# A retention layer with a mixture of experts on one Trainium2 core: the first step reordered over the engines, half-expert weights issued by ScalarE, and the tile numbers of the first groups computed in one part

## The chip, the cores and the metric

The kernel runs on one core of one Trainium2 chip. The metric is device time in microseconds (us); below, it is the median of several executions. A core has TensorE (PE; its weight loads are shown apart as PEld), VectorE (DVE), ScalarE (ACT), GpSimd (POOL) and SyncE (SP). Each engine works through its own list of instructions in order. Transfers are issued by SP, ACT or POOL, each on a queue of its own, and are carried by 16 DMA engines.

## The reference

For `x` of 2 x 2048 tokens and 256 features, in float32:

```python
x = x + attn(layernorm(x))      # gated linear attention, 4 heads of 64, decay per head
x = x + moe(layernorm(x))       # 8 experts, the best 2 of each token, 256 -> 1024 -> 256
```

The attention keeps a state W per head. With y the normalised input, v = y W_write^T, and y shifted by one token as the key, each chunk gives `reads = (y y_shifted^T * M) v + (W y) * g_p`, where M, g_p, g_w and g_C are powers of gamma = sigmoid(decay). The reads are scaled by alpha = exp(log_alpha), multiplied by W_read^T and added to the residual. The second part takes a softmax over 8 gate logits, picks the two best experts, and adds `p * (gelu(x w1 + b1) w2 + b2)` for each.

## The kernel before

**Order.** Everything is scheduled by hand: the order of the program text is the order of each engine's list. `attention(p)` (lines 404 to 510) is a generator for step p of 16; a step handles 128 tokens of both sequences. It yields seven times (k = 0 to 6), and the main loop (lines 920 to 940) puts other work into these places. From step 9 on the expert tiles are woven in; each `piece()` is one eighth of a tile of 128 token slots. After the 16 steps only tiles are left, so most of the kernel's time is the two matmul lines L853 (`ph`, first expert matrix) and L815 (`py`, second).

**One step.** On PE: `pv` (L414, values and gate logits from the transposed input yT), `pS` (L423, scores), `pO` of the step before (L392, the product with W_read), `pt` (L341, transposes for the next step), `pR` (L467 and L475, reads), `pW` (L495, the state's change). On DVE: `A` = pS times the decay mask (L429), the statistics of step p + 2 (L277 to L231), the addition of pO (L395), the new state (L500), `rg` (L354). On ACT: the copies v (L416), yT (L347) and rdT (L480), `wkg` (L365), the sum x (L322) and, for steps 1 to 10, the normalised y (L297). POOL raises the variance to the power -0.5 (L233), makes the masks and writes token rows to their experts' slots in DRAM (L523). SP moves y into the shifted copy wk (L309 to L311) and loads the next xin (L84).

**Start (lines 87 to 149 and 869 to 883).** xin(0), wwT and xin(1) are loaded by SP; decay, log_alpha, gateT, wrT and wr by ACT. The log decay needs an Exp and a Ln on ACT and small operations on DVE (L121 to L137); from it ACT makes the mask dmask (L140, four Exps), g_w, g_c and g_p (L146 to L149), and POOL cuts the mask (L142). `ps` (L872) sums the gate weights, and L876 centres them. Then come the statistics, y and transposes of step 0, the statistics of step 1, the rest of the mask, the sum x of step 0, `setup_rest` (lines 174 to 203, constants on POOL and three transfers on ACT) and the scaling of wrg by alpha (L883). `norm(1)` stands inside step 0, behind A.

**Expert weights.** The second matrices w2 stay in SBUF. SP issues them in 16 halves of 512 KB (L925), up to a count per step, `W2_BY = [2, 5, 8, 11, 14, 16]`. The first matrices w1c, 1 MB a tile, are loaded per tile by `ask_weights` (L753), and the token rows xg by `ask` (L764); both read the tile's numbers (expert and row) from SBUF into a register of SP first.

**Routing.** `route(q)` (L529) is a generator for a group of two steps. It yields 1 inside a woven part, whose next operation may be put anywhere between DVE's other operations by `beside()` (L251), and yields nothing at the end of a part. `advance()` (L886) finishes the woven part and starts the next. `dispatch(q)` (L679) computes the numbers of the tiles that are full after group q: 14 small DVE operations in five parts, one between each pair of slot writes. `EARLY` gives 9 tiles for q = 1, 8 after that. The tiles of a group are known to `ask_weights` when dispatch has ended, and to `ask` when the route has.

**PSUM.** The pool ps_m has three buffers that pv, pW, pK (L613), pg, ph and, from result 7 on, pO take in turn; whoever takes a buffer waits for the reader of the one before.

Of the kernel before, what the change touches and what calls it, by code (L numbers as in the profile page):

```python
# [46 lines left out]
def block_kernel(  # L47
# [68 lines left out]
    left = iota(one([P, 1], F32, "left"), [[0, 1]], P - 1, -1)  # L116

# [10 lines left out]
    nc.vector.tensor_scalar(neg, neg, 0.0, None, ALU.max)  # L128
    nc.vector.tensor_scalar(age, age, 0.0, None, ALU.max)

    def decays():

        nc.vector.tensor_scalar(lg, lg, 1.0, None, ALU.add)
        nc.scalar.activation(lg, lg, AF.Ln)
        yield
        nc.vector.tensor_tensor(lg, lg, neg, ALU.add)
        nc.vector.tensor_scalar(lg, lg, -1.0, None, ALU.mult)  # L137
        nc.vector.tensor_scalar(g_w, lg[:, 0:H], left, None, ALU.mult)
        for h in range(H):
            nc.scalar.activation(dmask[:, h % 2, h // 2, :], age, AF.Exp, scale=lg[:, h : h + 1])  # L140
        dmask4 = dmask.rearrange("p j g c -> p (j g) c")
# [4 lines left out]
        nc.scalar.activation(g_w, g_w, AF.Exp)  # L146
        nc.scalar.activation(g_c, lg[:, 4:6], AF.Exp, scale=float(P))
        for hh in range(2):
            nc.scalar.activation(g_p[:, hh, :], pos, AF.Exp, scale=lg[:, 4 + hh : 5 + hh])  # L149
        yield  # L150
# [23 lines left out]
    def setup_rest():  # L174
# [5 lines left out]
        nc.scalar.dma_start(slots[DUMMY : DUMMY + SB, :], empty)  # L180
        nc.scalar.dma_start(out[N : N + SB, :], empty[:, :D])
# [4 lines left out]
        )  # L186
        iota(ebase, [[RB, E]], 0, 0)
# [15 lines left out]
        nc.scalar.dma_start(b1_sb, b1)  # L203
# [80 lines left out]
    def norm(p):  # L284
# [10 lines left out]
        for b in range(B):  # L295
            if 0 < p < EASY + 2:
# [107 lines left out]
    def attention(p):  # L404
# [29 lines left out]
        if first:  # L434
            norm(1)
# [216 lines left out]
    def whole(n_f, n, name, ef, row, pick):  # L652
# [6 lines left out]
        yield  # L659
# [11 lines left out]
        yield  # L671
# [7 lines left out]
    def dispatch(q):  # L679

        n = EARLY[q]
        if not n:
# [8 lines left out]
        yield  # L691
# [4 lines left out]
        yield from whole(n_f, n, str(q), ef, t_row, hot)  # L696
        nc.vector.tensor_copy(t_e, ef)
        yield
# [311 lines left out]
```

## Time and profile before

| | |
|---|---|
| median of 5 executions | 647.01 us |
| lowest, highest | 644.19, 648.09 us |
| the profiled execution | 644.14 us |
| its span, first to last instruction | 642.4 us |
| time around the span | 1.74 us |
| mean granted TensorE clock | 0.991 of full speed |

The span is divided among the steps like this; the times are the starts of the first pv of each step.

| step | 0 | 1 | 2 | 3 | 4 | 5 | 6 | 7 | 8 | 9 |
|---|---|---|---|---|---|---|---|---|---|---|
| start of pv, us | 8.61 | 19.50 | 27.07 | 34.64 | 42.68 | 51.20 | 60.05 | 68.61 | 77.12 | 85.75 |

In the page, an engine's busy time stands beside its share of the span. A row of the timeline has the start, the duration, the engine, the line and the operation, the tile written and those read, and in brackets how long the engine had been idle and what ended that. A row of the windows has the busy time of each engine in a stretch of the span, the granted clock, the mean busy share of the DMA engines and the rate.

### The profile page before, as it was taken

How to read it: one execution, taken by the hardware profiler on the slowest of the kernel's cores; microseconds unless marked ns; L12 is line 12 of the kernel's file. 1: busy time of each engine (PE TensorE's matmuls, PEld its weight loads, DVE VectorE, ACT ScalarE, POOL GpSimd, SP SyncE). 2: the span in 40 equal slices, each digit the busy share in tenths (PEclk: the TensorE clock that was granted, in tenths of full speed). 3: DMA queues.
4: the chain of work that ended last, by engine and by line, in shares of the span. 5: the costliest groups of instructions: out<-in, count | busy, mean ns of one | idle time of the engine just before them, and what ended most of it. 6: DMA issues, size and time to landing. Idle time of an engine off the chain costs nothing. (4 is left out here: it accounts for less than half of the span.)

```text
span 642.4 us, 14995 instructions
## 1 busy us (share of the span) xinstructions
PE 619.5 (96%) x4706; PEld 561.8 (87%) x4706; DVE 261.4 (41%) x1141; ACT 288.9 (45%) x770; POOL 223.5 (35%) x198
## 2 busy tenths in 40 slices
PE   5999989999999999999999998999999999999995
PEld 3877779998999999999999998999999999999994
DVE  4588986346443464524542552222222222222220
ACT  5787763435334353434434443444444444443441
POOL 4016676416531256213641671211121122111121
PEclk9899989999999999999999999999999999999998
DMA  4789698946876567566766688776777667777741
GB/s 134 261 275 334 167 355 224 281 139 181 243 210 192 146 170 230 156 196 195 181 199 179 194 255 261 223 195 186 194 212 214 196 187 194 216 214 186 191 99 20
DMA packets 58720, 129.77 MB, mean 202 GB/s; under 512 B 7968, under 2 KB 43936, under 8 KB 50064
## 3 DMA queue, kind: packets, MB, share of 16 engines
q1 hardware_dynamic: 44384, 110.46, 56.7%
q0 software_dynamic: 12720, 17.47, 12.8%
q10 hardware_dynamic: 1536, 0.84, 0.4%
q8 instruction: 42, 0.69, 0.4%
q14 instruction: 38, 0.31, 0.2%
HBM read 101.54 MB, written 23.01 MB: 194 GB/s over the span
## 5 line engine op out<-in xcount | busy, mean ns | idle before, releaser
L853 PEld LDWEIGHTS ph<-xT,w1c 128*128 128x128 f32 x2144 | 317.3, 192 | 25.8 <-DVE xT L791 1.2
L853 PE MATMUL ph<-xT,w1c 128*128 128x128 f32 x2144 | 328.7, 276 | 1.0 <-DVE xT L791 1.0
L858 ACT ACTIVATE hT<-ph,b1c 128x128 f32<-128x128 f32 x536 | 196.8, 367 | 295.2 <-PE ph L853 293.1
L815 PE MATMUL py<-w_sb,hT 128*128 x1072 | 319.7, 380 | 0.0
L822 POOL DMA_INDIRECT out<-yo,dest x67 | 105.4, 1573 | 320.8 <-DMA out<-yo,dest 84.9
L815 PEld LDWEIGHTS py<-w_sb,hT 128*128 128x128 f32 x1072 | 163.0, 192 | 0.2
L821 DVE SCALAR_TENSOR_TENSOR yo<-py,wt,b2c 128x256 f32<-128x256 f32 x67 | 32.3, 483 | 240.4 <-PE py L815 238.8
L523 POOL DMA_INDIRECT slots<-pay,slot_i x64 | 63.2, 987 | 43.7 <-ACT wkg L365 15.7
L414 PE MATMUL pv<-wwg,yT 128*128 128x264 f32 x128 | 34.7, 412 | 3.1 <-DVE state L500 2.3
L392 PE MATMUL pO<-wrg,rdT 128*128 128x264 f32 x128 | 33.2, 392 | 0.0
L414 PEld LDWEIGHTS pv<-wwg,yT 128*128 128x128 f32 x128 | 24.4, 199 | 8.8 <-PE pv L414 3.5
L429 DVE TENSOR_TENSOR A<-pS,dmask 128x1024 f32<-128x1024 f32 x16 | 19.6, 1223 | 29.7 <-PE pS L423 29.7
L789 PE MATMUL px<-ident,xg 128*128 128x128 f32 x134 | 25.8, 275 | 3.7 <-DMA xg<-slots 3.0
L791 DVE COPY xT<-px 128x256 f32<-128x256 f32 x67 | 27.8, 415 | 1.8 <-PE px L789 1.7
L789 PEld LDWEIGHTS px<-ident,xg 128*128 128x128 f32 x134 | 18.8, 142 | 10.8 <-issue 2.1
L392 PEld LDWEIGHTS pO<-wrg,rdT 128*128 128x128 f32 x128 | 23.7, 190 | 4.4
L395 DVE TENSOR_TENSOR x<-x,pO 128x264 f32<-128x264 f32 x32 | 13.4, 426 | 31.5 <-PE pO L392 31.5
L803 DVE TENSOR_SCALAR b2c<-b2c,wt 128x256 f32<-128x256 f32 x67 | 24.6, 367 | 2.4
L233 POOL TENSOR_TENSOR rstd_a<-ve_a,expo 128x2 f32<-128x2 f32 x16 | 13.1, 819 | 27.7 <-DVE ve_a L231 16.0
L423 PEld LDWEIGHTS pS<-yT 64*128 64x128 f32 x256 | 15.6, 187 | 5.9 <-issue 3.5
L553 ACT ACTIVATE pay<-x,shift_b,rstd_b 128x256 f32<-128x256 f32 x32 | 19.0, 594 | 2.3 <-DVE shift_b L238 2.1
L500 DVE SCALAR_TENSOR_TENSOR state<-state,g_c,pW 128x128 f32<-128x128 f32 x30 | 9.2, 343 | 23.3 <-PE pW L495 23.0
(163 smaller groups left out, 430.7 us busy)
## 6 DMA issues: line engine op xcount, KB each, us to landing
w1c<-in_w SPq DMA_DIRECT2D x67, 1024.0 KB, 7.1
xg<-slots SPq DMA_DIRECT2D x67, 132.5 KB, 7.0
b2c<-in_b SPq DMA_DIRECT2D x67, 128.0 KB, 4.8
w_sb<-in_w SPq DMA_DIRECT2D x16, 512.0 KB, 5.4
xin<-in_x SPq DMA_DIRECT2D x16, 256.0 KB
out<-x SPq DMA_DIRECT2D x16, 256.0 KB, 2.2
wk<-y SPq DMA_DIRECT2D x16, 224.0 KB, 6.2
out<-yo,dest POOLq DMA_INDIRECT x67, 6.7
```

The source lines that it names most:

```text
L392: nc.tensor.matmul(pO, lhsT=rdTs[p][:, c, b * P : (b + 1) * P], rhs=wrg[:, c, :], start=(c == 0), stop=(c == 1))
L414: nc.tensor.matmul(pv, lhsT=yT[:, b, c, 1:], rhs=wwg[:, c, :], start=(c == 0), stop=(c == 1))
L429: nc.vector.tensor_tensor(A, pS.rearrange("p j (b g) -> p j b g", b=B), dmask.rearrange("p j g c -> p j (g c)").unsqueeze(2).to_broadcast( ...
L523: put = nc.gpsimd.indirect_dma_start(out=next(slot_views), out_offset=IndirectOffsetOnAxis(ap=index, axis=0), in_=rows, in_offset=None,)
L789: nc.tensor.transpose(px[:, c, :], xg[:, c * P : (c + 1) * P], ident)
L791: nc.vector.tensor_copy(xT, px)
L803: nc.vector.tensor_scalar(b2c, b2c, wt, None, ALU.mult)
L815: nc.tensor.matmul(r["py"], lhsT=hT, rhs=w2_sb[:, ds(r["at"], 1), fc * D : (fc + 1) * D].rearrange("p a d -> p (a d)"), start=(fc == 0), s ...
L821: nc.vector.scalar_tensor_tensor(yo, r["py"], r["wt"], r["b2c"], ALU.mult, ALU.add)
L822: add = nc.gpsimd.indirect_dma_start(out=next(out_views), out_offset=IndirectOffsetOnAxis(ap=r["dest"], axis=0), in_=yo, in_offset=None, c ...
L853: nc.tensor.matmul(ph, lhsT=r["w1c"][:, c, fc * P : (fc + 1) * P], rhs=r["xT"][:, c, :], start=(c == 0), stop=(c == 1),)
L858: mark[0] = nc.scalar.activation(hT, ph, AF.Gelu_apprx_tanh, bias=r["b1c"][:, fc : fc + 1]).ins.name
```

## The change

Seven things are changed. (1) The first loads are spread anew: xin(0) goes in two halves, one on SP and one on ACT; gateT stands ahead of decay and log_alpha on ACT; wrT and wr go to SP. (2) The decay's arithmetic moves: |decay| by an Abs on ACT in place of two DVE operations, the "+ 1" as the bias of the Ln, the clamp of `age` on POOL, and two DVE operations of the log become one. The Exps of g_w, g_c and g_p come ahead of POOL's cut of the mask. (3) `norm(1)` comes ahead of step 0, with y(1) on DVE, and the second call of `decays` ahead of the transposes of step 0. (4) `setup_rest` is split, and the sum x of step 0, the second half of the setup, the scaling of wrg and three transfers come inside step 0; the transfers go to SP. (5) 14 matmuls of the identity, whose result is not read, are put on PE: ten ahead of ps and four behind it. (6) The w2 halves are issued by ACT, from k = 4 of step 0 on. (7) The numbers of the tiles of q = 1, 2 and 3 are one woven part.

```diff
-    xins = {0: load_x(0)}
+    xins = {0: chk.tile([P, B, D], F32, tag="xin", name="xin_0", bufs=4)}
+    nc.sync.dma_start(xins[0][:, 0, :], x[0, 0:P, :])
+    nc.scalar.dma_start(xins[0][:, 1, :], x[1, 0:P, :])
+    nc.sync.dma_start(wwg[:, :, :D], wwT.rearrange("(c p) o -> p c o", p=P))
+    nc.scalar.dma_start(wwg[:, :, D:], gateT.rearrange("(c p) e -> p c e", p=P))
     nc.scalar.dma_start(dec, decay)
     nc.scalar.dma_start(lal, log_alpha)
-    nc.sync.dma_start(wwg[:, :, :D], wwT.rearrange("(c p) o -> p c o", p=P))
-    nc.scalar.dma_start(wwg[:, :, D:], gateT.rearrange("(c p) e -> p c e", p=P))
     xins[1] = load_x(1)
-    nc.scalar.dma_start(wrg[:, :, :D], wrT.rearrange("(c p) o -> p c o", p=P))
-    nc.scalar.dma_start(wr_sb, wr.rearrange("(c p) o -> p c o", p=P))
+    nc.sync.dma_start(wrg[:, :, :D], wrT.rearrange("(c p) o -> p c o", p=P))
+    nc.sync.dma_start(wr_sb, wr.rearrange("(c p) o -> p c o", p=P))
...
+    nc.gpsimd.tensor_scalar(age, age, 0.0, None, ALU.max)
...
-    nc.vector.tensor_scalar(neg, dec, -1.0, None, ALU.mult)
-    nc.vector.tensor_tensor(mag, dec, neg, ALU.max)
+    nc.scalar.activation(mag, dec, AF.Abs)
     nc.scalar.activation(lg, mag, AF.Exp, scale=-1.0)
     nc.scalar.activation(alpha, lal, AF.Exp)
-    nc.vector.tensor_scalar(neg, neg, 0.0, None, ALU.max)
-    nc.vector.tensor_scalar(age, age, 0.0, None, ALU.max)
+    nc.scalar.activation(lg, lg, AF.Ln, bias=1.0)
 
     def decays():
-        nc.vector.tensor_scalar(lg, lg, 1.0, None, ALU.add)
-        nc.scalar.activation(lg, lg, AF.Ln)
-        yield
-        nc.vector.tensor_tensor(lg, lg, neg, ALU.add)
-        nc.vector.tensor_scalar(lg, lg, -1.0, None, ALU.mult)
+        nc.vector.tensor_scalar(neg, dec, -1.0, 0.0, ALU.mult, ALU.max)
+        yield
+        nc.vector.scalar_tensor_tensor(lg, lg, -1.0, neg, ALU.mult, ALU.subtract)
         nc.vector.tensor_scalar(g_w, lg[:, 0:H], left, None, ALU.mult)
...
-            if 0 < p < EASY + 2:
+            if 1 < p < EASY + 2:
                 nc.scalar.activation(
...
         beside()
-        if first:
-            norm(1)
         if p + 2 < NC and p < EASY:
             norm_stats(p + 2)
         yield
         scaled_writes(p)
         if first:
+            sums(0)
             gate_products()
...
+        pause = 1 if 2 * (q + 1) < EASY else None
...
-        yield
+        yield pause
...
+    def warm_up(n, name):
+        pm = ps_m.tile([P, P], F32, tag="pm", name=f"warm_{name}")
+        for _ in range(n):
+            nc.tensor.matmul(pm, lhsT=ident, rhs=ident, start=True, stop=True)
+
+    warm_up(10, 0)
     ps = ps_m.tile([P, E], F32, tag="pm", name="ps")
     for c in range(2):
         nc.tensor.matmul(ps, lhsT=ones, rhs=wwg[:, c, D:], start=(c == 0), stop=(c == 1))
+    warm_up(4, 1)
     norm_stats(0)
     next(start)
     norm(0)
+    next(start)
     nc.vector.scalar_tensor_tensor(wwg[:, :, D:], by_e(ps, 2), -1.0 / D, wwg[:, :, D:], ALU.mult, ALU.add)
     transposes(0)
+    setup = setup_rest()
+    next(setup)
+    next(start)
     norm_stats(1)
-    next(start)
-    sums(0)
-    setup_rest()
-    for c in range(2):
-        nc.vector.tensor_scalar(wrg[:, c, :D], wrg[:, c, :D], alpha[:, c : c + 1], None, ALU.mult)
+    norm(1)
+
+    def behind_first():
+        next(setup)
+        for c in range(2):
+            nc.vector.tensor_scalar(wrg[:, c, :D], wrg[:, c, :D], alpha[:, c : c + 1], None, ALU.mult)
+        nc.sync.dma_start(slots[DUMMY : DUMMY + SB, :], empty)
+        nc.sync.dma_start(out[N : N + SB, :], empty[:, :D])
+        nc.sync.dma_start(b1_sb, b1)
...
         for k, _ in enumerate(attention(p)):
-            if k in (0, 2, 3, 4) and halves < W2_BY[p]:
+            if p == 0 and k == 0:
+                behind_first()
+            if (p or k > 3) and k in (0, 2, 3, 4, 5) and halves < W2_BY[p]:
                 e, j = divmod(halves, 2)
                 js = slice(j * FC * D // 2, (j + 1) * FC * D // 2)
-                nc.sync.dma_start(w2_sb[:, e, js], w2[e, :, js])
+                nc.scalar.dma_start(w2_sb[:, e, js], w2[e, :, js])
```

The five plain yields between the parts of `dispatch` and `whole` become `yield pause`.

More of the change, by code (lines that the diff above doesn't have):

```diff
@@ L140, in decays @@
             nc.scalar.activation(dmask[:, h % 2, h // 2, :], age, AF.Exp, scale=lg[:, h : h + 1])
+        nc.scalar.activation(g_w, g_w, AF.Exp)
+        nc.scalar.activation(g_c, lg[:, 4:6], AF.Exp, scale=float(P))
+        for hh in range(2):
+            nc.scalar.activation(g_p[:, hh, :], pos, AF.Exp, scale=lg[:, 4 + hh : 5 + hh])
+        yield
         dmask4 = dmask.rearrange("p j g c -> p (j g) c")
@@ L145, in decays @@
         )
[L146 to L149, printed above, removed]
         yield
@@ L179, in setup_rest @@
         nc.gpsimd.tensor_scalar(empty[:, ROW - 1 : ROW], pcol, float(N), None, ALU.add)
-        nc.scalar.dma_start(slots[DUMMY : DUMMY + SB, :], empty)
-        nc.scalar.dma_start(out[N : N + SB, :], empty[:, :D])
         nc.gpsimd.memset(before, 1.0)
@@ L186, in setup_rest @@
         )
+        yield
         iota(ebase, [[RB, E]], 0, 0)
@@ L202, in setup_rest @@
         nc.gpsimd.memset(base_e, 2.718281828459045)
-        nc.scalar.dma_start(b1_sb, b1)
+        yield
     slot_views = iter(dram_disjoint_views(slots, 2 * N // P + E + NTILE))
@@ L650, in block_kernel, with whole @@
     tiles, found, known = [], [], []
-    def whole(n_f, n, name, ef, row, pick):
+    def whole(n_f, n, name, ef, row, pick, pause=None):
         upto = sml.tile([P, E], F32, tag="upto", name=f"upto_{name}")
@@ L670, in whole @@
         nc.vector.tensor_tensor(pick, wide(ef, E), by_e(e_of, n), ALU.is_equal)
-        yield
+        yield pause
         nc.vector.tensor_tensor(tmp, pick, by_e(origin, n), ALU.mult)
@@ L690, in dispatch @@
         nc.vector.tensor_copy(n_f, n_i)
-        yield
+        yield pause
         t_e = one([P, n], I32, f"t_e_{q}")
@@ L695, in dispatch @@
         ef = sml.tile([P, n], F32, tag=f"ef{n}", name=f"ef_{q}", bufs=1)
-        yield from whole(n_f, n, str(q), ef, t_row, hot)
+        yield from whole(n_f, n, str(q), ef, t_row, hot, pause)
         nc.vector.tensor_copy(t_e, ef)
-        yield
+        yield pause
         got = sml.tile([P, E], F32, tag="got", name=f"got_{q}")
```

## The prediction

> **What bounds the kernel now.** I read the engine table first, then the windows, then the timeline of the start and of the step at which the expert tiles begin.
>
> ```profile
> PE 619.5 (96%) x4706; PEld 561.8 (87%) x4706; DVE 261.4 (41%) x1141; ACT 288.9 (45%) x770; POOL 223.5 (35%) x198
> ```
>
> PE is busy for 96% of the span. From the first expert matmuls at 91.50 us it stands idle for 2.5 us (0.7 and 1.8 us before px). So a microsecond saved ahead of 91.5 us comes off the end, as long as the order of PE's list stays; nothing that the change touches makes PE's list after that shorter. The time is to be won in two places. The first is step 0:
>
> ```profile
> 3.96 0.75 DVE L277 BATCH_NORM_STATS2 st<-xin 128x6 f32<-128x256 f32 x2
> 8.61 3.89 PE L414 MATMUL pv<-wwg,yT 128*128 128x264 f32 x8 [0.78 <-DVE yT L344]
> 12.43 1.19 PE L423 MATMUL pS<-yT 64*128 64x128 f32 x16
> 13.73 1.23 DVE L429 TENSOR_TENSOR A<-pS,dmask 128x1024 f32<-128x1024 f32 x1 [3.03 <-PE pS L423]
> 15.71 1.18 PE L341 MATMUL pt<-ident,y 128*128 128x128 f32 x4 [1.11 <-ACT y L297]
> 16.83 1.97 PE L475 MATMUL pR<-A,v 128*64 128x128 f32 x16
> ...
> 19.50 2.05 PE L414 MATMUL pv<-wwg,yT 128*128 128x264 f32 x8
> ```
>
> Step 0 takes 10.89 us from pv to pv (8.61 to 19.50), though step 1 with more work takes 7.57. The reader is to see two things. PE waits for y(1), which is made only behind A; and PE is slow: the eight pv take 3.89 us here and 2.05 at 19.50, pR 1.97 and 1.09 later (33.15). The granted clock of 16 to 19 us is 0.50. It prints as 1.00 before 15 us, yet the durations say half speed there until about 12.4. The second place:
>
> ```profile
> 90.10 0.44 PE L789 MATMUL px<-ident,xg 128*128 128x128 f32 x2 [1.22 <-DMA xg<-slots]
> ...
> 91.50 2.90 PE L853 MATMUL ph<-xT,w1c 128*128 128x128 f32 x12 [0.95 <-DVE xT L791]
> ```
>
> PE waits 1.22 us for the first token rows and 0.95 for xT and its first register load; then the clock of 91 to 95 us is 0.51, 0.50, 0.50, 0.78, which costs 1.7 us (the sum of what is missing).
>
> **The first loads.** The statistics start at 3.96, behind four DVE operations from 3.21 on. Without these they start when xin(0) is there: not before 3.2 (decay, 3 KB, landed 2.4 us after its issue at 0.81), not after 3.96. I take 3.3. From the statistics to the first transpose took 2.75 us (3.96 to 6.71), so pt stands at 6.05 and ends at 7.2.
>
> But decay and log_alpha are now third and fourth on ACT's queue, issued at about 1.70 and 2.15, and alpha's Exp stands ahead of the Ln. From alpha's Exp to the end of Ln took 1.71 us (4.68 to 6.39, a table load of 1.28 in it). Landing 2.4 us after the issue, as decay did, log_alpha is there at 4.55 and Ln is done at 6.3: hidden, because y(0) ends at 6.3. Landing 3.95 us after it, as gateT did (1.74 to 5.69), it is there at 6.1 and Ln is done at 7.8. Then DVE, in order, holds lg, g_w, the centring (0.2 + 0.23 + 0.17) and the copy yT (0.69) behind it, and pv starts at 9.1 where the first case gives 7.95. gateT is the nearest row, a small transfer behind others on this queue, and there are 128 KB more ahead; I weigh it four to one. An Abs was not on ACT before; it costs 0.2 like the Exps beside it, or 1.28 more should it bring a fourth table load. "ScalarE: Activation LUTs" of the Trainium skill (Table sets: the hidden batching unit) has abs in every set, so no load; no run here shows it.
>
> wrT and wr, behind xin(1) on SP, are first used at some 14 us; everything loaded at the start had come by 6.5 us (the DMA share falls to 0.03 in 7 to 8), so they are hidden, as is the clamp of age on POOL (0.29 like L183, done by 2.5, used after 7).
>
> **From pv to the next pv.** If pv starts at 9.1 and the clock is as before: pv until 13.0, pS until 14.1, A from 14.2 to 15.45. Beside A PE now has pg (1.06) and pt(1) (0.6 at full clock), done by 15.8, since y(1) is early: dmask from the second Exp table's end (7.8 + 1.28) to 10.4, POOL's cut 0.64, the power 0.77, shift and y(1) on DVE 1.0, together 13.0. pR at 15.85 and then 1.49 us to pv as in later steps (33.15 to 34.64): pv(1) at 17.35, 2.15 us sooner. ScalarE is no later: v by 13.8, wkg 1.26, x 1.09, then yT(1) by 16.9. With pv at 7.95 the same sum gives pv(1) at 16.15, 3.35 sooner. Weighed, **-2.4 us**. What hides the rest of the setup is PE: POOL's second half (about 2 us) and DVE's wrg are not waited for before pO at 22.
>
> **The identity matmuls.** Four 128-column matmuls take 1.12 us at the slow clock (6.71), so ten last from 1.5 to about 3.7 and four 0.9 more behind ps. They delay nothing, since gateT lands later. Bounds: 0, or pv at 2.05 instead of 3.89, -1.8. I take 0, the row that exists being pv at half speed after transposes without a gap over 0.8 us.
>
> "TensorE: Matmul & The Clock Gate" of the Trainium skill (Part 1) says that full clock comes after a window of some 3.4 us of sustained work, and that PE falls back after an idle one. Both slow stretches here last about 3.4 us, which agrees; but they follow idle times of only 1.1 and 2.2 us, so the trace is stricter. By the rule ten matmuls with a wait behind them fill no window, and this term is 0; were the rule wrong here it would be -1.8.
>
> **w2 on ScalarE.** SP's 16 issues took 0.47 us each (median), up to 1.01. Three a step add 1.4 us to ACT, which is busy 5.1, 5.3, 7.6, 5.3 and 7.7 us of steps 1 to 5 (7.57, 7.57, 8.04, 8.52, 8.85 long). In even steps ACT waits 1.15 us for pt and 1.05 for pR at just these places: hidden. In step 3 two issues stand ahead of yT(4); 0.4 us go into its wait for L573, and the copy ends at 42.7 instead of 42.1, when pv starts at 42.68. The second half of pv waits there for the state until 44.55 anyway. Cost 0; +1 if the cover goes. SP's list gets shorter, but no PE wait of these steps ends on an SP load.
>
> "Trainium Kernel Development and Optimization" of the Trainium skill (Key Constraints) has it that all issuing queues share the same 16 DMA engines, and that a second one only saves issue time. By that rule neither the split xin(0) nor w2 moves any byte sooner. DMA shares of 0.82 to 0.98 in steps 1 to 5 agree.
>
> **One woven part.** In step 6 the numbers of the first tiles are then known at k = 0 instead of k = 4, ahead of wk(8) and xin(10) on SP, so w1c of tiles 0 and 1 (issued 76.45 and 78.14, 7 us to land) leave some 5 us sooner, into a stretch with a DMA share of 0.09 to 0.45 (70 to 74). xg, issued at 81.9 and 8.2 us on its way, has less ahead of it. The price is on DVE: eleven operations of 0.22 us, 2.4 us, now stand in one go ahead of L395. In step 6 nobody waits. In step 8 pv(9) takes the PSUM buffer of pO(7), whose reader moves from 83.79 to about 86.4:
>
> ```profile
> 83.79 0.42 DVE L395 TENSOR_TENSOR x<-x,pO 128x264 f32<-128x264 f32 x1
> ...
> 85.75 2.05 PE L414 MATMUL pv<-wwg,yT 128*128 128x264 f32 x8
> ```
>
> So pv(9) waits until 86.9, 1.1 us: a new wait in place of the 1.22 us for xg. A(9) and xT follow it, and ph starts 0.5 us later than now, but the idle time is in two pieces. I take it that the slow stretch then goes: +0.5 - 1.7 = **-1.2 us**. Bounds: +0.6 (clock as now) and -3.9 (no idle time and full clock). For q = 3, 14 operations (3.1 us) go in one piece at 105.0, ahead of xT (105.47), which ph needs at some 108.2: **+0.3**, from 0 to 0.5.
>
> **Sum.** -2.4 - 1.2 + 0.3 = -3.3: an execution like the profiled one (span 642.4 and 1.74 around it, 644.14) would take 640.8. The median of the runs, 647.01, stands 2.87 above it, and I let that distance be: 643.7. No change is within 0.5% (3.2 us), about what a measurement of this kernel can tell.
>
> **Rivals.** (1) The Ln chain and the new PSUM wait eat it: pv at 9.6, pv(1) -1.6, clock as now +0.6, q = 3 +0.5: -0.5, 646.5. For it: ACT's order, gateT's 3.95 us. Against: y(1) is off PE's path in any case. (2) Everything early: -3.35 at the start, -1.8 for the warm clock but only -1.0 of that since A waits for the mask, -2.6 at the tiles: -7, 640. For it: decay's 2.4 us. (3) ScalarE is held by its w2 issues: they are in order, ahead of yT, rdT and wkg, while the DMA engines are 0.82 to 0.98 busy. ACT has 9.5 us free in steps 1 to 5 and gets 14 issues; at 1.2 us each they take 16.8, 7.3 too much: +4.0 after the gain, 651. It outweighs the gain from 0.91 us an issue. SP's longest speaks for it, the median of 0.47 against.
>
> **Chances.** Forecast 0.52, rival 1 0.24, rival 2 0.13, rival 3 0.11. The range 640.0 to 648.0 takes in the first three and leaves rival 3 and a tail out. The forecast straddles the 0.5% bound: faster by more, 0.35 of its 0.52 and rival 2, 0.48; slower 0.10; within 0.42.
>
> **What would show it.** pv(1) at 17.4 (right) or 19 (wrong); DVE idle ahead of lg for Ln; pv(0) still 3.9 us long; pv(9) waiting for L395; no clock of 0.50 after the first ph; w2 issues of 0.5 us on ACT, yT not behind them. An xg that lands after PE asks for it, or a clock lost elsewhere, would make the sum wrong.

## The result, and the profile after

The changed kernel takes **648.67 us** (median of 28 runs, 646.10 to 652.55); the kernel before takes 645.95 us (54 runs). The ratio is **1.0048, 95% interval 1.0035 to 1.0061**: slower by about 3.1 us, where I had forecast 3.3 us less. The profiled execution has a span of 649.3 us (642.4 before) and so shows a loss of 6.9 us, more than the typical one. Sizes are therefore taken from ratios below, and places from traces. Line numbers are those of the changed kernel, for most lines one less than before (pv L413, pO L391, A L428, the sum with pO L394); pv(p) is the first pv of step p.

The engine table of the page after:

```profile
PE 624.3 (96%) x4734; PEld 565.6 (87%) x4734; DVE 264.1 (41%) x1138; ACT 288.1 (44%) x769; POOL 225.3 (35%) x199
```

PE has 28 records more (the fourteen identity matmuls, two records each) and still 96%. Nothing in shares and sums tells what happened; it takes the timelines. The first is PE's in step 0, after:

```profile
1.45 4.64 PE L875 MATMUL warm<-ident 128*128 128x128 f32 x20 [1.45 <-POOL ident masks.py:199]
...
9.75 2.05 PE L413 MATMUL pv<-wwg,yT 128*128 128x264 f32 x8 [1.43 <-DVE yT L343]
11.73 1.16 PE L422 MATMUL pS<-yT 64*128 64x128 f32 x16
...
15.06 1.09 PE L473 MATMUL pR<-A,v 128*64 128x128 f32 x16 [0.69 <-ACT yT L345]
...
16.54 2.05 PE L413 MATMUL pv<-wwg,yT 128*128 128x264 f32 x8
```

The first step gained: pv(0) starts 1.1 us later than before (decay landed at 6.46, Ln behind it, yT behind Ln), but it takes 2.05 us instead of 3.89, and pv(1) starts at 16.54 instead of 19.50. The second is ACT's, in steps 1 and 2:

```profile
23.04 0.33 ACTq L945 DMA_DIRECT2D w_sb<-in_w  x1
23.42 0.20 ACT L345 COPY yT<-yT 128x4 f32<-128x4 f32 x1 [1.95 <-DMA wk<-y]
...
26.58 0.34 ACTq L945 DMA_DIRECT2D w_sb<-in_w  x1
26.95 0.59 ACT L478 COPY rdT<-pR 128x512 f32<-128x512 f32 x1 [2.85 <-DMA wk<-y]
```

An issue takes 0.33 us, as small as I said. But ACT was idle for 1.95 and 2.85 us ahead of the two copies, the issue included, until a transfer wk<-y landed that neither the copy of yT nor that of rdT reads: the issue ahead of them waits, and they stand behind it. PE then waits 1.39 us for rdT ahead of pS. The third is PE's in steps 7 to 9:

```profile
77.70 0.67 PE L465 MATMUL pR<-rg,state 64*64 64x128 f32 x16 [0.83 <-DVE A L428]
80.81 0.42 PE L612 MATMUL pK<-both,before 128*128 128x40 f32 x2 [0.52 <-DVE both L590]
...
83.47 1.13 PE L413 MATMUL pv<-wwg,yT 128*128 128x264 f32 x4 [1.01 <-DVE state L498]
88.90 2.13 PE L391 MATMUL pO<-wrg,rdT 128*128 128x264 f32 x4 [2.12 <-ACT v L415]
94.09 2.05 PE L413 MATMUL pv<-wwg,yT 128*128 128x264 f32 x8
98.98 1.60 PE L853 MATMUL ph<-xT,w1c 128*128 128x128 f32 x12 [1.39 <-DVE xT L791]
```

The waits for A and for v are nowhere in the trace of before. From pv(7) to pv(9) it was 17.14 us; now it is 22.78. The wait for v leads to ACT's sums, which waited for the buffer x1 of two groups earlier to be written out:

```profile
86.14 1.09 ACT L321 ACTIVATE x<-xin,shift_a,up 128x256 f32<-128x256 f32 x2 [4.92 <-DMA out<-x]
```

### The profile page after: what moved, and what is told of

It reads as the page before. It is cut to its first block, busy times and chain, and to the rows that moved or that the text cites. A ratio compares the mean times of both kernels' runs of the same rounds, so it can differ in the third digit from the quotient of the medians.

```text
span 649.3 us, 15048 instructions
## 1 busy us (share of the span) xinstructions
PE 624.3 (96%) x4734; PEld 565.6 (87%) x4734; DVE 264.1 (41%) x1138; ACT 288.1 (44%) x769; POOL 225.3 (35%) x199
## 5 line engine op out<-in xcount | busy, mean ns | idle before, releaser
L413 PE MATMUL pv<-wwg,yT 128*128 128x264 f32 x128 | 33.8, 404 | 3.9 <-DVE state L498 2.5
L391 PE MATMUL pO<-wrg,rdT 128*128 128x264 f32 x128 | 35.4, 411 | 2.1 <-ACT v L415 2.1
L428 DVE TENSOR_TENSOR A<-pS,dmask 128x1024 f32<-128x1024 f32 x16 | 19.6, 1224 | 32.3 <-PE pS L422 32.3
L413 PEld LDWEIGHTS pv<-wwg,yT 128*128 128x128 f32 x128 | 23.8, 194 | 9.1 <-PE pv L413 3.6
L391 PEld LDWEIGHTS pO<-wrg,rdT 128*128 128x128 f32 x128 | 24.8, 200 | 7.4 <-ACT v L415 2.5
L394 DVE TENSOR_TENSOR x<-x,pO 128x264 f32<-128x264 f32 x32 | 13.3, 427 | 32.2 <-PE pO L391 32.0
L422 PE MATMUL pS<-yT 64*128 64x128 f32 x256 | 19.5, 294 | 1.4 <-ACT rdT L478 1.4
```

What stands on the lines that cost most here:

```text
L391: nc.tensor.matmul(pO, lhsT=rdTs[p][:, c, b * P : (b + 1) * P], rhs=wrg[:, c, :], start=(c == 0), stop=(c == 1))
L413: nc.tensor.matmul(pv, lhsT=yT[:, b, c, 1:], rhs=wwg[:, c, :], start=(c == 0), stop=(c == 1))
L422: nc.tensor.matmul(pS[:, j, (2 * b + hh) * P : (2 * b + hh + 1) * P], lhsT=yT[r, b, hh, 0:P], rhs=yT[r, b, hh, 1:], start=True, stop=True,)
```

## The experiments

This table holds the starts on PE (us, from the timelines) of kernels that ran where the kernel before took 645 to 646 us. e4, e9 and e17 ran there too and follow below; the profile of e4 is of an execution 8 us over its median (651.85 us). Labels e1 to e18 are those of the runs below.

| kernel | pv(1) | pv(4) | pv(7) | pv(9) | 7 to 9 | first ph | ratio to before (95%) |
|---|---|---|---|---|---|---|---|
| before | 19.50 | 42.68 | 68.61 | 85.75 | 17.1 | 91.50 | 1 |
| after | 16.54 | 43.38 | 71.31 | 94.09 | 22.8 | 98.98 | 1.0048 (1.0035 to 1.0061) |
| e1: after, w2 on SP | 15.62 | 39.38 | 65.31 | 86.76 | 21.5 | 91.66 | 1.0019 (0.9998 to 1.0040) |
| e2: after, not woven | 16.03 | 42.25 | 68.19 | 85.31 | 17.1 | 90.47 | 0.9974 (0.9949 to 1.0000) |
| e3: first step alone | 15.74 | 39.34 | 65.27 | 82.40 | 17.1 | 88.06 | 0.9955 (0.9933 to 0.9977) |
| e11: before, w2 on ACT | 19.90 | 43.25 | 69.68 | 86.81 | 17.1 | 91.97 | 0.9969 (0.9946 to 0.9991) |
| e12: e1, three x1 | 15.50 | 39.73 | 67.24 | 88.64 | 21.4 | 93.84 | 1.0000 (0.9976 to 1.0023) |
| e10: e3, decay first | 14.81 | 38.07 | 64.02 | 81.14 | 17.1 | 86.30 | 0.9946 (0.9921 to 0.9972) |
| e18: e10, woven, weights behind | 14.97 | 39.16 | 65.10 | 84.94 | 19.8 | 90.15 | 1.0018 (0.9990 to 1.0046) |

The runs e5 to e8 and e13 to e16 fell where the kernel before took 661 to 663 us: there PE stands idle in many places without a releaser in the trace (up to 5 us at a time), and the intervals are 0.7 to 0.9% wide. What differed isn't known: under chip number 8 the kernel before took 662.74 us beside e5 to e8 and 646.33 us beside e17 and e18. In the expectations a counted pv is meant by the time in brackets beside it.

### The three parts, taken apart

My theory after the traces was that ACT's waits cost 3 to 5 us and SP's new order the rest.

```diff
-                nc.scalar.dma_start(w2_sb[:, e, js], w2[e, :, js])
+                nc.sync.dma_start(w2_sb[:, e, js], w2[e, :, js])
```

> The changed kernel with the 16 halves of w2 issued by SyncE again, at the same places of the program. Theory (ScalarE is held at its w2 issues, each of which waits until an older transfer that shares its completion counter has landed, and that is mostly a SyncE transfer such as wk<-y): the waits of yT, rdT and the row copy for wk<-y on ScalarE go, the fifth pv starts near 50 us (54.8 in the changed kernel, 51.2 in the kernel before), and the time falls by 3 to 5 us against the changed kernel: ratio to the kernel before 0.997 to 1.000. Rival a (the w2 bytes crowd the DMA engines whichever queue issues them, and a later first step only shows it): no change, ratio 1.004 to 1.006. Rival b (the loss is all in steps 6 to 9, behind the woven part; what ScalarE loses is caught up by then): ratio 1.003 to 1.005 and the ninth pv still near 94 us.

Measured: 1.0019; pv(4) at 39.38 instead of 43.38, pv(5) at 47.90 instead of 54.76, and none of ACT's waits behind a w2 issue. Against the changed kernel this is 0.0029 (1.9 us), at the edge of what the two intervals tell apart: less than the theory's 3 to 5, more than rival a. What came early was given away again between pv(7) and pv(9), the place that rival b names; its figures don't fit (pv(9) at 86.76 and not near 94).

```diff
-        pause = 1 if 2 * (q + 1) < EASY else None
+        pause = None
```

> The changed kernel with the numbers of the first tiles spread over the steps again (no pause of 1 for the early parts); w2 stays on ScalarE. Theory (w1c and b2c of tiles 0 and 1 stand ahead of out<-x of step 5 on SyncE, so the buffer x1 comes free late, and ScalarE's sums, v and pO wait behind it): out<-x is issued some 8 us sooner, ScalarE's wait of 4.9 us for it goes, pO no longer waits 2.1 us for v, and the time falls by 1.5 to 4 us: ratio to the kernel before 0.999 to 1.002. Rival (the eleven operations in one go on VectorE are the loss, SyncE's order is none): the same fall, but out<-x is awaited as before. Rival (the woven part gains, as predicted): the time rises by about 1 us, ratio 1.006.

Measured: 0.9974, 0.0074 (4.8 us) less than the changed kernel, more than any theory gave. The woven part costs most; pv(7) to pv(9) is 17.1 us again, and ACT no longer waits for out<-x.

Both edits together:

> Both undone: w2 on SyncE and the numbers spread, so that only the reordered first step is left of the change. Theory: the second pv starts near 16.5 us (19.5 before), nothing later takes it away, and the time is 2 to 3.3 us under that of the kernel before: ratio 0.995 to 0.997. Rival (the steps up to the first expert tiles are bound by DMA, so that an early first step is given back by 60 us): ratio 0.999 to 1.001 with the ninth pv at 85 us as before.

Measured: 0.9955, 643.08 us. pv(1) at 15.74 and the first ph at 88.06, 3.4 us sooner than before: what the first step wins isn't given back. Going back by the rows, of the 0.0048 the first step has -0.0045 (-2.9 us), w2 on ACT +0.0019 (+1.2 us, alone within the intervals) and the woven part +0.0074 (+4.8 us). Going back over e1 instead of e2, they are +0.0029 and +0.0064 (1.9 and 4.1 us).

```diff
-                nc.sync.dma_start(w2_sb[:, e, js], w2[e, :, js])
+                nc.scalar.dma_start(w2_sb[:, e, js], w2[e, :, js])
```

in the kernel before, and nothing else:

> The kernel before with nothing changed but the queue of w2: ScalarE issues its 16 halves at the places where SyncE did. Theory (ScalarE waits at them): slower by 2 to 5 us, ratio 1.003 to 1.008, with waits of yT, rdT or the row copy behind a w2 issue. Rival (it costs only together with the early first step, when ScalarE has no slack): within 1 us, ratio 0.9985 to 1.0015. My prediction's term for it was 0, or +1 us.

Measured: 0.9961 (0.9938 to 0.9985): faster, which nobody had expected. Again, for the trace:

> The kernel before with w2 on ScalarE and nothing else, a second time, for its trace: it measured 0.9961 (0.9938 to 0.9985), where a loss was expected, and the first profile (650.2 us at a clock of 0.982) doesn't show where 2.5 us are won. If the gain is real: 0.994 to 0.998, and the trace shows an earlier first ph than 91.5 us, since SyncE, free of w2, issues wk and out<-x sooner. If it was chance: 0.998 to 1.003 and pv and ph where they stand in the kernel before.

Measured: 0.9969 (0.9946 to 0.9991). The gain is there twice. Where it is won I can't show: in its trace pv(1) to pv(9) and ph are 0.4 to 1.1 us later than in the profile of before, and that profile (644.14 us) is itself a quick one of its kernel. What can be said is that the issues on ACT cost nothing when the first step is long; with the short one they cost 0.0019 to 0.0029, about as much as the intervals are wide.

### What w2 costs on ScalarE: the issue, or the wait ahead of it

The first step alone, with a copy on ACT at each of the 16 places:

```diff
                 nc.sync.dma_start(w2_sb[:, e, js], w2[e, :, js])
+                nc.scalar.copy(spent, ident)
```

> The first step alone with w2 on SyncE, and on ScalarE, at each place where a half of w2 is issued, a copy of 128x128 into a tile that nobody reads (about 0.35 us, as long as an issue). It computes nothing that the output needs. Theory (the price of w2 on ScalarE is the wait ahead of the issue, not the 16 x 0.35 us that they occupy): within 0.0015 of the first step alone, pv of steps 1 to 4 within 0.3 us of 15.7, 23.3, 30.9, 39.3. Rival (rival 3 of the prediction: the issues' own time): as with w2 on ScalarE, fifth pv 2 to 3 us later.

Measured: 0.9958 (0.9915 to 1.0001); pv(1) to pv(4) at 15.77, 23.34, 30.91, 39.75. Time on ACT of nearly an issue's length (a copy took 0.30 us) costs nothing by pv(3) and 0.4 to 0.6 us at pv(4) (30.88 and 39.34 in e3, 31.08 and 39.18 in e14, the same kernel without copies), and from pv(1) to pv(4) two executions of one kernel differ by as much (23.80 us in e5, 24.26 in e13). Beside it, the same kernel with the issues on ACT:

> The first step and w2 on ScalarE, not woven, a second time. Theory (ScalarE stands at its w2 issues until an older transfer has landed, and the short first step leaves no slack for it): 0.001 to 0.004 more than the first step alone on this chip, and the fourth and fifth pv 1 to 3 us later (30.9 and 39.3 with w2 on SyncE). Rival (w2 on ScalarE gains, as it did alone): 0.002 to 0.004 less than the first step alone.

Measured: 0.9986 (0.9948 to 1.0024); pv(2) to pv(4) at 23.76, 32.16, 41.76: 0.4, 1.3 and 2.0 us later than with the copies, ACT again idle for 2.15 and 2.23 us where an issue stands. The medians can't tell the two apart here; by the traces it isn't the issue's length, as rival 3 of the prediction had it, but the wait. What an issue waits for stands in the program's semaphores, which the trace keeps: the transfers of both queues share eight completion counters, and a transfer waits until the one that had its counter before has landed. For the w2 issue of the changed kernel at 26.58 us, in program order:

```
SP    wk(2) <- y(2)     counter 5   (third transfer on it)   after ACT's y(2)
ACT   half 5 of w2      counter 5   waits until counter 5 shows three landed
ACT   rdT(1)            behind it in ACT's list
```

Counter 5 showed three landed at 26.55 us. Of the sixteen w2 issues in this trace eight start 0.02 to 0.03 us after the landing that they wait for, six times that of an SP transfer and twice that of an earlier half of w2. With w2 on SP (e1, e3) no wait of ACT between 18 and 60 us ends on a transfer; on ACT they hold up PE, through yT and rdT.

The base of these two, again:

> The first step alone, a second time, as the base of the three others on this chip: 0.994 to 0.997 as before (0.9955, 0.9933 to 0.9977). A second ratio over 0.998 would mean that the gain of the first step isn't firm.

Measured: 0.9979 (0.9940 to 1.0019), pv(1) at 15.95. The ratio lies just under the limit of 0.998 that I had set, and the interval holds 1: by itself this run doesn't confirm the gain, though it doesn't speak against 0.9955 either.

In the reordered step w2 also starts later (k = 4 instead of 0). With the early start, on ACT, not woven:

```diff
-            if (p or k > 3) and k in (0, 2, 3, 4, 5) and halves < W2_BY[p]:
+            if k in (0, 2, 3, 4, 5) and halves < W2_BY[p]:
```

> First step reordered and w2 on ScalarE, numbers not woven (ratio 0.9974 so far), but the first two halves of w2 are issued at k = 0 and 2 of the first step as in the kernel before, not at k = 4 and 5. Theory (w2 on ScalarE costs where its issues fall behind a transfer of SyncE that is still on its way, and the later start of w2 in the changed kernel crowds steps 1 to 3): pv of step 4 near 39.5 to 40.5 us (42.25 with the later start, 39.34 with w2 on SyncE), ratio 0.993 to 0.996. Rival (ScalarE is held in steps 1 to 3 in any case now that the first step is short): pv of step 4 still near 42, ratio 0.996 to 0.999.

Measured: 1.0012 (0.9970 to 1.0054); pv(1) 17.55, pv(2) and pv(3) 7.57 us apart, undisturbed, then pv(4) at 42.77. The waits have moved (2.23 us ahead of yT(1), 2.42 us ahead of yT(4)) and not gone: pv(4) is where the rival has it, though the ratio decides nothing.

### What the woven part costs: SyncE's order, or the operations on VectorE

My theory was SP's order: w1c of tiles 0 and 1 now ahead of out<-x(5), whose buffer ACT's sums wait for. The weights behind it again, w2 on SP:

```diff
-            ask_weights_on(stream["piece"] // FC + 2)
+            if p != 6 or k >= 4:
+                ask_weights_on(stream["piece"] // FC + 2)
```

> First step and woven part as in the changed kernel, w2 on SyncE, but the weights of tiles 0 and 1 are asked for only from the place k = 4 of step 6 on, behind out<-x(5), wk(8) and xin(10), as in the kernel before. So the eleven VectorE operations still stand in one piece, and SyncE's order is the old one. Theory (SyncE's order is the loss): 2.5 to 4.5 us less than with the weights ahead (646.97 there), ratio to the kernel before 0.994 to 0.998, as with the first step alone (0.9955); no wait of ScalarE for out<-x. Rival (the burst on VectorE ahead of the sums x is the loss): ratio 1.000 to 1.003 as with the weights ahead.

> First step and woven part, w2 on SyncE, the weights of tiles 0 and 1 asked for behind out<-x(5), wk(8) and xin(10): a second time, beside the first step alone. If SyncE's order is the whole loss of the woven part: within 0.0015 of the first step alone (which was 0.9955), and the ninth pv between 82 and 83.5 us. If the burst on VectorE has a part of it: 0.002 to 0.004 more than the first step alone, ninth pv at 84 us or later.

Measured: 0.9961 (0.9926 to 0.9996) and 0.9952 (0.9911 to 0.9994). That seemed to settle it for SP's order. But pv(7) to pv(9) was 21.5 and 19.8 us in these traces, with 0.8 to 1.0 us of PE's waiting for A still there; and it was 22.3 us in e16 on the same chip as e13, which isn't woven. There something else sets these steps. The other side of the theory, three buffers with the weights ahead:

```diff
-            x1s[q] = grp.tile([P, G, D + E], F32, tag="x1", name=f"x1_{q}")
+            x1s[q] = grp.tile([P, G, D + E], F32, tag="x1", name=f"x1_{q}", bufs=3)
```

> The other side of the same: first step and woven part as in the changed kernel, the weights ahead of out<-x(5) on SyncE, w2 on SyncE, but three buffers for x1 where there were two, so that ScalarE's sums need not wait until out<-x(5) has been read out. Theory (the loss passes through the buffer x1): ScalarE's wait of 5.2 us for out<-x and PE's of 2.4 us for v go, ratio 0.994 to 0.998, though out<-x is as late as with the weights ahead. Rival (the weights' 2 MB crowd the transfers of these steps, or SyncE's stand at the register load holds wk(8) and xin(10)): xin(10) and xg still come late, ratio 0.999 to 1.003.

> First step, woven part and w2 on SyncE, three buffers for x1, a second time, since the first interval (0.9940 to 1.0032) held both theories. Theory (the loss of the woven part passes through the buffer x1 that out<-x frees late): 0.994 to 0.998, no wait of ScalarE for out<-x, ninth pv near 82 to 84 us (86.8 with two buffers, 82.4 without the woven part). Rival (SyncE's later order costs through xin and xg as well): 0.999 to 1.002.

Measured: 0.9986 (0.9940 to 1.0032), and then 1.0000 (0.9976 to 1.0023). ACT's wait for out<-x is gone, and the loss stays: pv(9) is at 88.64, of which the profile loses some 1.7 us to the clock (0.50 from 80 to 82 us), and the ratio is far from 0.9955. The theory falls here. The deciding run, on the best first step and where before took 646 us, has the weights behind and the operations in one piece:

> The first step with decay first, w2 on SyncE, the numbers of the first tiles in one woven part, the weights asked for behind out<-x(5), wk(8) and xin(10). If the burst on VectorE costs nothing: 0.993 to 0.9965, as without it (0.9946, 0.9921 to 0.9972), eighth and ninth pv near 72.5 and 81.1 us. If it costs 1 to 2 us of its own (A, the sums x and with them pv of step 8 wait behind it): 0.996 to 0.999 and the ninth pv at 82.3 us or later.

Measured: 1.0018 (0.9990 to 1.0046) against 0.9946 without weaving: +0.0072, 4.7 us, with SP's order as before; against e17, which ran beside it and isn't woven either, +0.0067. In the medians SP's order has no part that shows (e1 against e3: +0.0064); in the traces pv(7) to pv(9) takes 21.5 us in e1 and 19.8 in e18, so a part of 1.6 us isn't excluded. DVE's timeline in step 6 shows the price. First with the operations in one piece (e18), then spread (e10):

```profile
60.72 1.22 DVE L428 TENSOR_TENSOR A<-pS,dmask 128x1024 f32<-128x1024 f32 x1
...
64.41 0.23 DVE L670 TENSOR_TENSOR tmp<-hot,origin 128x72 f32<-128x72 f32 x1
64.68 0.23 DVE L673 TENSOR_REDUCE first<-tmp 128x9 f32<-128x72 f32 x1
64.94 0.17 DVE L675 SCALAR_TENSOR_TENSOR t_row<-jj,first 128x9 int32<-128x9 f32 x1
...
65.50 0.77 DVE L394 TENSOR_TENSOR x<-x,pO 128x264 f32<-128x264 f32 x2
...
67.17 0.17 DVE L230 TENSOR_SCALAR ve_b<-mv 128x4 f32<-128x4 f32 x1
...
69.66 0.19 DVE L546 TENSOR_TENSOR pL<-x,rstd_b 128x32 f32<-128x32 f32 x1 [0.79 <-POOL rstd_b L232]
...
70.22 1.22 DVE L428 TENSOR_TENSOR A<-pS,dmask 128x1024 f32<-128x1024 f32 x1
```

```profile
59.63 1.22 DVE L428 TENSOR_TENSOR A<-pS,dmask 128x1024 f32<-128x1024 f32 x1
...
62.06 0.42 DVE L394 TENSOR_TENSOR x<-x,pO 128x264 f32<-128x264 f32 x1
...
64.41 0.20 DVE L230 TENSOR_SCALAR ve_b<-mv 128x4 f32<-128x4 f32 x1
...
64.75 0.23 DVE L670 TENSOR_TENSOR tmp<-hot,origin 128x72 f32<-128x72 f32 x1
64.90 0.15 DVE L329 TENSOR_TENSOR std<-ve_a,rstd_a 128x2 f32<-128x2 f32 x1
65.01 0.23 DVE L673 TENSOR_REDUCE first<-tmp 128x9 f32<-128x72 f32 x1
65.16 0.16 DVE L331 TENSOR_SCALAR std<-std 128x2 f32<-128x2 f32 x1
65.28 0.17 DVE L675 SCALAR_TENSOR_TENSOR t_row<-jj,first 128x9 int32<-128x9 f32 x1
...
66.96 0.18 DVE L546 TENSOR_TENSOR pL<-x,rstd_b 128x32 f32<-128x32 f32 x1
...
67.51 1.22 DVE L428 TENSOR_TENSOR A<-pS,dmask 128x1024 f32<-128x1024 f32 x1
```

From A(6) to A(7) it is 9.50 us against 7.88, for the same operations. So it is in every trace of this set: 9.50 or 9.51 in the woven kernels (after, e1, e12, e18), 7.87 to 7.89 in those without weaving (before, e2, e3, e9, e10, e11, e17). Two things make it up.

The first is GpSimd's power, which makes rstd_b from ve_b and for which DVE stands 0.79 us in e18. In e10 it begins 0.29 us after ve_b (at 64.70) and takes 1.04 us, and seven operations of the numbers lie over it. In e18 those are done, and it begins 1.03 us after ve_b (at 68.20), behind a slot write that runs from 67.22, and takes 1.43 us. With the numbers in one part, four slot writes stand on GpSimd between A(6) and the power where three stood. At e10's times the power would be over at 68.5, before DVE has got to L546 at 68.9: so it is the place on GpSimd that costs, and not only the operations that are gone from above it. Why it takes 1.43 us isn't shown.

The second, the other 0.83 us, is the piece itself: each of its operations needs the one before, and they start 0.26 us apart (64.41, 64.68, 64.94). In e10 they do so too (64.75, 65.01, 65.28), but L329 and L331, which need nothing of them, start in between.

PE, in e18:

```profile
71.49 0.67 PE L465 MATMUL pR<-rg,state 64*64 64x128 f32 x16 [0.84 <-DVE A L428]
74.59 0.41 PE L612 MATMUL pK<-both,before 128*128 128x40 f32 x2 [0.53 <-DVE both L590]
...
77.26 1.13 PE L413 MATMUL pv<-wwg,yT 128*128 128x264 f32 x4 [1.01 <-DVE state L498]
...
84.94 2.02 PE L413 MATMUL pv<-wwg,yT 128*128 128x264 f32 x8 [0.96 <-DVE x L394]
```

Step 7 takes 10.0 us instead of 8.5 (A, both and the state late), step 8 takes 9.8 instead of 8.6 (pv(9) waits for L394): 2.7 us, and q = 3 adds a wait of 0.8 us for xT that only the woven kernels have. That is 3.5 us; the three pairs of medians say 4.1 to 4.8, and what makes up the rest isn't shown.

### The first step, and whether more is to be had

The first step alone without the fourteen identity matmuls:

```diff
-    warm_up(10, 0)
...
-    warm_up(4, 1)
```

> The first step alone (w2 on SyncE, numbers not woven), without the fourteen identity matmuls ahead of and behind ps. Theory (they hold the clock up: pv of step 0 took 2.05 us instead of 3.89 in the changed kernel): pv of step 0 takes 3.0 to 3.9 us again and the second pv starts 0.5 to 1.8 us later than 15.7; time +0.5 to +1.8 us, ratio 0.9965 to 0.9985. Rival (my prediction's term of 0: they change nothing): ratio as with the first step alone, 0.9945 to 0.9965.

Measured: 0.9979 (0.9938 to 1.0019), which holds both. The trace, though of its slowest execution (666.23 us), decides for the theory in the first step:

```profile
8.86 3.89 PE L413 MATMUL pv<-wwg,yT 128*128 128x264 f32 x8 [1.05 <-DVE yT L343]
12.67 2.08 PE L422 MATMUL pS<-yT 64*128 64x128 f32 x16
...
17.77 1.60 PE L413 MATMUL pv<-wwg,yT 128*128 128x264 f32 x6
```

pv(0) takes 3.89 us and pS 2.08 again (2.05 and 1.16 with them), and pv(1) starts at 17.77 instead of 15.74 (e3) or 15.95 (e14): the fourteen matmuls are worth 1.8 to 2.0 us, about half of the 3.8 us that e3 wins by pv(1).

Decay first on ACT's queue:

```diff
+    nc.scalar.dma_start(dec, decay)
     nc.scalar.dma_start(xins[0][:, 1, :], x[1, 0:P, :])
     nc.scalar.dma_start(wwg[:, :, D:], gateT.rearrange("(c p) e -> p c e", p=P))
-    nc.scalar.dma_start(dec, decay)
...
-    nc.scalar.activation(alpha, lal, AF.Exp)
     nc.scalar.activation(lg, lg, AF.Ln, bias=1.0)
...
+        nc.scalar.activation(alpha, lal, AF.Exp)
         nc.scalar.activation(g_w, g_w, AF.Exp)
```

> The first step alone, with decay as the first load of ScalarE's queue instead of the third, log_alpha last, and alpha's Exp behind those of the decay. Theory (the statistics, lg and the copy yT on VectorE wait for decay, which landed at 6.5 us in the changed kernel): Ln is done by 6 us, the first pv starts at 7.9 to 8.4 us (8.95 now) and the second 0.4 to 1 us sooner than 15.7; time 0.4 to 1 us less, ratio 0.993 to 0.9955. Rival (xin(0), now behind decay on the queue, is as late as decay was): first pv between 8.7 and 9.5, ratio as with the first step alone.

Measured: 642.31 us, **0.9946 (0.9921 to 0.9972), the fastest kernel here by ratio**; Ln is done at 6.00, pv(0) starts at 8.23 and pv(1) at 14.81, 0.9 us sooner than in e3. The same first step has pv(1) at 14.97 in e18 and 15.16 in e17, that of e3 at 15.41 to 16.44 in the other traces that have it with w2 on SP. The traces show the step; the time alone couldn't tell it from 0.9955. It beats the kernel before and, with its interval, the changed one (1.0035 at least).

With w2 on SP from the first step's k = 0 on:

```diff
-            if (p or k > 3) and k in (0, 2, 3, 4, 5) and halves < W2_BY[p]:
+            if k in (0, 2, 3, 4) and halves < W2_BY[p]:
```

> The first step with decay first (0.9946 so far), w2 on SyncE, numbers not woven, but w2 from k = 0 and 2 of the first step on, as in the kernel before, not from k = 4. Theory (the DMA share is 0.36 between 10 and 20 us and about 1 from 30 to 60 us, so earlier halves take load off the steps that are full): pv of steps 4 and 5 0.5 to 1.5 us sooner than 38.07 and 46.58, ratio 0.992 to 0.995. Rival (these steps aren't held by transfers when SyncE issues w2): pv within 0.3 us of that, ratio 0.9935 to 0.9965. Rival (wk(1) and xin(3) come late behind 1 MB): second pv or the third later than 14.8 and 22.4 by over 0.5 us.

Measured: 0.9951 (0.9922 to 0.9981); pv(1) to pv(9) within 0.4 us of the run without it (pv(0) is 0.8 us later), the first rival. When SP issues w2, it makes no difference where it starts.

Identity matmuls also at the first expert tile, on the first step alone:

```diff
+        if stream["piece"] == 0:
+            ph = ps_m.tile([P, SB], F32, tag="pm", name="ph_0_0")
+            for _ in range(3):
+                nc.tensor.matmul(ph, lhsT=ident, rhs=ident, start=True, stop=True)
...
+            for _ in range(5):
+                nc.tensor.matmul(ph, lhsT=ident, rhs=ident, start=True, stop=True)
```

> The first step alone (w2 on SyncE, numbers not woven), with eight identity matmuls more at the first expert tile: three ahead of px, where TensorE waits for xg (0.83 us in the profile of the first step alone), and five between px and the first ph, where it waits for xT (1.26 us). Theory (short idle times of about 1 us are what takes the clock to half for 3.4 us; work in them keeps it): the first twelve ph take 1.60 us instead of 2.70, no clock under 0.9 between 88 and 92 us, time 1.0 to 1.7 us under the first step alone, ratio to the kernel before 0.9925 to 0.9945. Rival (the clock falls anyway, or the eight delay px and ph): the same or up to 1 us more, 0.9950 to 0.9975.

Measured: 0.9965 (0.9947 to 0.9983), no gain over 0.9955. The clock was 1.00 throughout 84 to 94 us, as the theory has it, and PE lost the time again elsewhere:

```profile
86.87 0.44 PE L789 MATMUL px<-ident,xg 128*128 128x128 f32 x2 [1.04 <-DMA xg<-slots]
88.46 1.38 PE L859 MATMUL ph<-ident 128*128 128x128 f32 x10 [1.15 <-issue]
89.67 1.50 PE L861 MATMUL ph<-xT,w1c 128*128 128x128 f32 x12
```

The five matmuls behind px didn't start until 1.15 us after it, beside the time in which xT was made, and then stood 1.2 us ahead of ph. The first ph starts at 89.67 instead of 88.06.

## Why the prediction was wrong, point by point

**What bounds the kernel: right.** The places were the first step and the tiles' beginning, and PE's idle time and clock there came through to the end (e3: 3.4 us at the first ph, 2.9 us in the median).

**The first loads: right in kind.** I weighed the Ln chain behind decay's load as four to one, with pv(0) at 9.1; it came at 9.75 in the profile of after, at 8.95 in e3 and at 8.23 with decay first. In after decay itself landed at 6.46 us, 4.7 us after its issue, where my nearest row had 3.95; in e3 it was there at 4.72, and log_alpha at 6.04. DVE did idle ahead of lg (1.10 us) for Ln. Three table loads stand on ACT (2.78, 7.06, 8.84), as many as before; Abs uses the one that Exp uses and brings no fourth, so the Trainium skill's "ScalarE: Activation LUTs" (Table sets) agrees with the trace.

**From pv to pv, and the identity matmuls: right sign, two sizes off.** I had -2.4 for the first and 0 for the second. pv(1) came 2.96 us sooner (3.8 in e3). The step that failed is "ten last from 1.5 to about 3.7". The sum was off already, since ten at four in 1.12 us last 2.8 us; and they lasted to 6.09, since each of these float32 matmuls is two records in the trace (ten are x20) and a transpose, from which I took the price, is one (four are x4). So PE worked from 1.45 on, for 4.64 us by these ten alone, and pv ran at full speed. "TensorE: Matmul & The Clock Gate" of the Trainium skill (Part 1) wants some 3.4 us of sustained work. Here the matmuls come 0.21 us apart until 6.4 us in e3 and 6.9 in after, and then 0.11: full speed came 4.9 and 5.5 us after the first, and in e8 PE worked from 8.86 to 14.68, 5.8 us, before it came. None of these traces has it after less than 3.4 us, and it was my length that made the term 0. The -1.8 that I named as its bound is about what e8 measured.

**w2 on ScalarE: "Cost 0; +1 if the cover goes".** The size was near: 0.0019 to 0.0029, 1.2 to 1.9 us with the short first step, of which the first lies within the intervals and the second at their edge. The reason was wrong. I compared busy time with free time, and e16 shows that this sum does cost next to nothing. What I left out is what the issue waits for: a counter that it shares with SP's transfers. Of "no PE wait of these steps ends on an SP load" nothing was left when ACT stood behind wk<-y. Rival 3 had the victim right (yT and rdT) and the mechanism wrong (1.2 us an issue; it was 0.33). The Trainium skill's rule that a second queue only saves issue time ("Trainium Kernel Development and Optimization", Key Constraints) is not all there is: here the second queue moved a wait from SP to ACT.

**One woven part: -1.2 and +0.3, measured +4.1 to +4.8.** This is the term that turned the sign, and the step in it that failed is "In step 6 nobody waits". I priced eleven operations at their 0.22 us, for step 8, and took it that the same work in another order costs step 6 nothing. But DVE was busy 26.8 of the 28 us from 60 to 88 in the profile of before, so it set the pace there as much as PE did. The old order had the numbers' small operations between others that don't need them and over GpSimd's power; in one piece they show their dependences (0.83 us), the power stands behind one slot write more with nothing over it (0.79 us), and A, both, state and then L394 are late: 1.5 us in step 7, 1.2 us in step 8. The new wait of pv(9) that I had found, 1.1 us, came as predicted (0.96 in e18, 0.95 in e12; in after and e1 the wait of pO for v, 2.12 and 2.37 us, stands in its place). For q = 3 the wait for xT is 0.8, not 0.3. The gain failed as well. Weights asked for 6.6 us sooner (67.01 in e1, 73.61 in e18) are awaited by nobody. PE's wait for xg ahead of the first px is gone, but since PE comes later: xg was issued at 80.11 in e1 and 82.39 in e18, against 78.79 in e3 and 77.63 in e10. The half-clock stretch of -1.7 went in the profiles of after and e1 (first twelve ph in 1.60 us), stayed in e18 (2.77), and went in e17 without weaving (1.60); in two executions of one kernel it stayed and went (2.81 in e6, 1.60 in e12). So it can't be put down to the order.

**Sum.** -2.9 + 1.2 + 4.8 = +3.1 instead of -2.4 + 0 - 1.2 + 0.3 = -3.3.

Left open: where w2 on ScalarE gains 0.3 to 0.4% with the old first step; how much of its loss with the new one is certain; and why the woven part shows no loss in e5 and e13, where PE stands without a releaser in the same steps. My reading is that those stalls cover it. For it: from A(6) to A(7) four of the five kernels without weaving take 9.05 to 9.11 us there (e7, e8, e14, e15; e16 7.94), so that the 9.51 of e5 and e13 is only 0.4 us more. That this is the whole of it isn't shown.

## What to carry to other kernels

An engine that is 95% busy in a stretch can set the pace there, whatever its share of the span. An order that puts independent operations between dependent ones is worth what the chain's gaps cost without them; and what is moved on one engine moves the places on the others (here a slot write ahead of GpSimd's power). Price the order, on every engine that the part touches, and not the sum of durations. Before a DMA moves to the queue of an engine that computes, read what its issue will wait for in the program, and who stands behind it in that engine's list. Matmuls on a constant paid at the start, where they filled the time up to the first real ones (e8); beside a wait on the path they were in the way (e9).

## What the runs showed of the hardware

- A DMA issue of ACT took 0.33 us, but ACT was idle for up to 2.85 us with one in it (from 24.10 to 26.95 us in after), waiting for a transfer that SP had issued; in this program eight completion counters serve both queues.
- Small DVE operations that each need the one before start 0.26 us apart; one that needs nothing of its neighbour starts 0.08 us after it (65.28, 65.36, 65.44 in e10), for the same 0.17 us of busy time.
- The clock doesn't fall with every gap. In e1 PE idled 2.37 us, and 1.39 us ahead of ph, with a granted clock of 1.00 from 60 to 100 us; in e12, with gaps of 0.84, 0.53 and 1.01 us, it fell to 0.50 for 80 to 82 us; in e18 the same three gaps (0.84, 0.53 and 1.01 us) left it at 1.00 from 70 to 90 us.
- The kernel before took 645 to 646 us in some sets of runs and 661 to 663 in others, 646.33 and 662.74 under the same chip number. In the second kind PE idles without a releaser: in the profile of e16 9.6 us in three waits ahead of ph and 5.3 us in seven ahead of pW, where that of e3 has none.
